# TensorE transposes instead of diagonal products: the B term of a selective scan on one core

## The chip, the cores and the metric

One Trainium2 chip; the program runs on one of its cores. The metric is the device time of one execution in microseconds, and the median of three runs is given. The core has five engines that run side by side, each through its own queue in order, and that wait for one another by semaphores: TensorE (PE, whose weight loads have a row of their own, PEld), VectorE (DVE), ScalarE (ACT), GpSimd (POOL) and SyncE (SP), which here only issues DMAs.

## The reference

The reference runs four layers over x of shape (4, 64, 64, 128), all in fp32. Layers 0, 1 and 3 are state-space blocks: a norm, a projection to 256 channels, a 3x3 depthwise convolution and SiLU, and then a selective scan in four directions (K = 4) over the 4096 positions of each image, with N = 16 states a channel. Layer 2 is a gated block without a scan. The scan is what matters here, cut to its core:

```python
def step(h, t):
    x_t, d_t, B_t, C_t = t
    h = jnp.exp(d_t[..., None] * A) * h + (d_t * x_t)[..., None] * B_t[:, :, None, :]
    return (h, jnp.einsum('bkdn,bkn->bkd', h, C_t))
```

So each state n needs, for every channel and position, a decay exp(delta*A), an input (delta*x)*B_n, a running recurrence along the positions, a product with C_n, and a sum over n.

## The kernel before, in words

The 4096 positions are cut into chunks of 512 (`CH`), channels lie on 128 partitions in two halves m. There are 12 turns (two pairs of images, three scan layers, one image a turn), each with 4 directions of 8 chunks: 384 chunks. A chunk has 8 periods: a period is one channel half and one group of four states (`place`, L879, picks both), so there are 3072 periods, and nearly all of the time is made of them.

In one period, states 0 and 1 of the group are side 0 and states 2 and 3 side 1. The recurrence is a VectorE scan (`scan`, L918), four a period, 512 positions each. The two sides get their input (delta*x)*B in two ways:

- Side 0 (`diagonals` L885, `pair_db` L895). delta*x stands transposed in SBUF (`duT`, positions on partitions). ScalarE builds diagonal matrices of B: ident times a column of B, 128x128, for each of four blocks of positions and each of two states, interleaved in one tile `diag`. TensorE multiplies `duT` by the diagonals: four products of 128x256 a period, into the PSUM tile `dbp` of two banks, in which the two states alternate element by element. The scans read it with a step of two.
- Side 1 (`lift` L915, L1048, L1049). ScalarE copies delta*x into a PSUM tile `dv` ("lifts" it). VectorE multiplies it by two rows of B, which a DMA has spread over all partitions (`bb`). The second product is written in place; the first goes into the other one of two `dv` tiles, and that one becomes the target of the next lift when its scan has read it.

Round this: ScalarE makes the decays (`decay` L903, two instructions a side) and saves the last column of a scan as the state for the next chunk (`save`). GpSimd multiplies the scans' results by C (`times_c` L934, 128x1024 each, twice a period, and in every second period adds the two sides). TensorE sums these over n into `yp` by products with ident (`add_up` L940). `leave` (L955) adds `yp` to the output when a half of a chunk is done.

The order on each queue is the order of the program text; nothing is moved by a scheduler. The loop over periods (from L985) sets it. In period i it issues the decay of side 0 of the next period (`then`), the save of the last one, the two scans of side 0, `times_c`, in even periods one `add_up`, `pair_db` of the next period, the decay of side 1 of the next period, the save, the two products at L1048 and L1049, the two scans of side 1, `times_c`, `lift` of the next period, half of a later group's diagonals, and two or three `add_up` of the period before. So TensorE's products for period i+1 are issued in the middle of period i, and the `add_up` calls of period i-1 near the end of period i. One more thing shapes this order: TensorE's `add_up` waits for GpSimd, which comes after VectorE.

Two other streams are woven in. `prologue` (L814) prepares the next chunk: loads, small products, delta, delta*x on GpSimd (L859), its transposes on TensorE (L865) and ScalarE's copies into `duT` (L867). It is cut by `yield` into ten steps, and `PIECES` says at which of the 16 half periods of a chunk the next step is issued. `other` feeds in the steps of the work between layers (norms, convolution, projections), spread by costs.

Of the kernel before, what the change touches and what calls it, by code (L numbers as in the profile page):

```python
# [13 lines left out]
F32 = mybir.dt.float32  # L14
AF = mybir.ActivationFunctionType
# [10 lines left out]
CH = 512  # L26
NCH = L // CH
RPC = CH // W
P = 128
WP = W + 2  # L30

CQ = 4
# [1 line left out]
PAIRED = (0, 2, 4, 6)  # L34


PIECES = (0, 3, 4, 6, 8, 9, 10, 11, 12, 13)


_VSS = [  # L40
# [58 lines left out]
def vss_stack_kernel(ctx: ExitStack, tc: tile.TileContext, x: bass.AP, weights, out: bass.AP, n_batch=B, layers=(0, 1, 2, 3)):  # L99
# [6 lines left out]
    nc = tc.nc  # L106
# [4 lines left out]
    ident = const.tile([P, P], F32, name="ident")  # L111
# [14 lines left out]
    for i in layers:  # L126
# [14 lines left out]
        t = const.tile([P, small_n + VSS_N - tail_at], F32, name=f"w{i}")  # L141
# [27 lines left out]
    def cols(c):  # L169
        return slice(c * CH, (c + 1) * CH)  # L170
# [596 lines left out]
    for turn, (e, i) in enumerate(turns):  # L767

        for nth, k in enumerate((1, 3, 0, 2) if turn else (0, 1, 3, 2)):
            for ci in range(NCH):  # L770
                s = SimpleNamespace(turn=turn, e=e, v=wt[i], layer=i, nth=nth, k=k, ci=ci)
                s.c = NCH - 1 - ci if k >= 2 else ci
                s.columns, s.back = k % 2 == 1, k >= 2
                s.end = 0 if s.back else CH - 1
                s.step = slice(None, None, -1 if s.back else 1)
                s.first, s.last = ci == 0, ci == NCH - 1
                s.flip = len(chunks) % 2
                s.diag, s.cb, s.bb, s.h, s.hc = {}, {}, {}, {}, {}
                chunks.append(s)
    per_turn = K * NCH  # L780

# [27 lines left out]
    def scans(pool, ring, deep, psum):  # L809
# [4 lines left out]
        def prologue(s):  # L814


            lane, v = lanes[s.e % 2], s.v
            s.xs = ring.tile([P, 2, CH], F32, tag="xs", name="xs")
            nc.sync.dma_start(out=s.xs, in_=(lane.x_col if s.columns else lane.x_row)[:, :, cols(s.c)])
            if s.first:  # L820
                s.dt = pool.tile([R, DI], F32, tag="dt", name="dt_w")
                nc.sync.dma_start(out=s.dt, in_=weights[s.layer][1][:, s.k * DI : (s.k + 1) * DI])


            s.xd_d = lane.xd[s.k % 2][s.c]
            s.xd = pool.tile([2 * NX, CH], F32, tag="xd", name="xd")
            if s.back:
                nc.sync.dma_start(out=s.xd[:NX], in_=s.xd_d[1])
            yield
            if s.back:  # L830
                yield
            else:
                ps = psum.tile([P, CH], F32, tag="misc", name="ps_x")
                for m in range(2):
                    nc.tensor.matmul(ps[: 2 * NX], v["xp"][:, s.k % 2, m, :], s.xs[:, m], start=(m == 0), stop=(m == 1))
                yield
                nc.scalar.copy(s.xd, ps[: 2 * NX])
            s.delta = pool.tile([P, 2, CH], F32, tag="delta", name="delta")
            halves = (s.flip, 1 - s.flip)
            for m in halves:  # L840
                ps = psum.tile([P, CH], F32, tag="misc", name="ps_dt")
                nc.tensor.matmul(ps, s.dt[:, m * P : (m + 1) * P], s.xd[:R], start=True, stop=True)  # L842
                yield
                func = AF.Identity if m == halves[0] else AF.Softplus
                nc.scalar.activation(s.delta[:, m], ps, func, bias=v["dtb"][:, s.k, m : m + 1])  # L845
            m = halves[0]
            nc.scalar.activation(s.delta[:, m], s.delta[:, m], AF.Softplus)  # L847
            nc.scalar.preload_act_table_set("natural_log_exp_and_others")
            ps = psum.tile([P, 4, NX], F32, tag="misc", name="ps_bt")
            for j in range(4):  # L850
                nc.tensor.transpose(ps[:, j, :], s.xd[:NX, j * P : (j + 1) * P], ident[:NX, :NX])
            yield
            if not s.back:
                nc.sync.dma_start(out=s.xd_d.rearrange("k r t -> (k r) t"), in_=s.xd)
            s.bt = pool.tile([P, 4, N], F32, tag="bt", name="bt")
            nc.scalar.copy(s.bt, ps[:, :, R : R + N])
            s.du = pool.tile([P, 2, CH], F32, tag="du", name="du")
            for m in halves:
                nc.gpsimd.tensor_mul(s.du[:, m], s.delta[:, m], s.xs[:, m])  # L859
                yield  # L860
            s.duT = pool.tile([P, 4, 2, P], F32, tag="duT", name="duT")
            for m in halves:
                ps = psum.tile([P, 4, P], F32, tag="misc", name="ps_duT")
                for j in range(4):
                    nc.tensor.transpose(ps[:, j, :], s.du[:, m, j * P : (j + 1) * P], ident)  # L865
                yield
                nc.scalar.copy(s.duT[:, :, m, :], ps)  # L867
            yield
# [10 lines left out]
        def place(s, i):  # L879


            q = i // 2
            return q, (i + q + s.flip) % 2

        def diagonals(s, q, half):  # L885

            if half == 0:
                s.diag[q] = pool.tile([P, 4, P, 2], F32, tag="diag", name="diag")
            for t in (2 * half, 2 * half + 1):
                for j in range(2):  # L890
                    nc.scalar.activation(  # L891
                        s.diag[q][:, t, :, j], ident, AF.Copy, scale=s.bt[:, t, CQ * q + j : CQ * q + j + 1]
                    )

        def pair_db(s, i):  # L895
            q, m = place(s, i)
            s.db = psum.tile([P, CH, 2], F32, tag="dbp", name="dbp")
            for t in range(4):
                nc.tensor.matmul(  # L899
                    s.db[:, t * P : (t + 1) * P, :], s.duT[:, t, m, :], s.diag[q][:, t], start=True, stop=True  # L900
                )

        def decay(s, i, side):  # L903
            q, m = place(s, i)
# [8 lines left out]
        dv = [psum.tile([P, CH], F32, name=f"dv{j}") for j in range(2)]  # L913

        def lift(s, i):  # L915
            nc.scalar.copy(dv[i % 2], s.du[:, place(s, i)[1]])  # L916

        def scan(s, i, side, j, da, db):  # L918
            q, m = place(s, i)
            if j == 0:  # L920
                s.h[i, side] = deep.tile([P, 2, CH], F32, tag="h", name="h")
            n = CQ * q + 2 * side + j
            init = 0.0 if s.first else s.state[:, m, n : n + 1]
            nc.vector.tensor_tensor_scan(  # L924
                s.h[i, side][:, j, s.step], da[:, j, s.step], db[:, s.step], init, ALU.mult, ALU.add
            )
# [13 lines left out]
        def add_up(s, i, *calls):  # L940


            q, m = place(s, i)
            start, end = (0, 7) if m == s.flip else (1, 6)
            for call in calls:
                opens = i == start and call == (2 if i in PAIRED else 0)
                if opens:
                    setattr(s, f"yp{m}", psum.tile([P, CH], F32, tag=f"yp{m}", name="yp"))
                side, j = divmod(call, 2)
                closes = i == end and call == 3  # L950
                nc.tensor.matmul(getattr(s, f"yp{m}"), ident, s.hc[i, side][:, j], start=opens, stop=closes)  # L951
                if closes:
                    full.append((s, m))
# [15 lines left out]
        for step in sum([combine(0, psums)] + opening[:4], []):  # L969
            step()  # L970
        s = chunks[0]
        pro = prologue(s)
        for _ in pro:
            pass
        for q, half in ((0, 0), (0, 1), (1, 0)):
            diagonals(s, q, half)
        spread(s, 0, 0)
        spread(s, 0, 1)
        pair_db(s, 0)
# [1 line left out]
        da = [decay(s, 0, side) for side in range(2)]  # L981
# [3 lines left out]
        for at, (s, i) in enumerate(periods):  # L985
            then = periods[at + 1] if at + 1 < len(periods) else None
            if i == 0:
                nxt = chunks[at // 8 + 1] if at // 8 + 1 < len(chunks) else None
# [14 lines left out]
            def piece(number):  # L1003

                if nxt and number in PIECES:
                    next(pro)
# [21 lines left out]
                save(*before, 1)  # L1028
            if spreads:
                spread(*spreads, 0)  # L1030
            scan(s, i, 0, 0, da[0], s.db[:, :, 0])
            other(0)
            scan(s, i, 0, 1, da[0], s.db[:, :, 1])
            times_c(s, i, 0)

            if before and i % 2 == 0:
# [10 lines left out]
            du, db = dv[i % 2], dv[1 - i % 2]  # L1047
# [3 lines left out]
            other(2)  # L1051
            scan(s, i, 1, 1, da[1], du)
            times_c(s, i, 1)
            if then:
                lift(*then)

            q, half = (i + 2 + i % 2) // 2, 1 - i % 2
            if q < 4:
                diagonals(s, q, half)
            elif nxt:  # L1060
                diagonals(nxt, q - 4, half)
            if i < 2 and full:
                leave(*full.pop(0))
            if before:
                add_up(*before, *((2, 3) if i % 2 else (1, 2, 3)))
            piece(2 * i + 1)
            other(3)
            da = da_next
# [103 lines left out]
```

## Time and profile before

| what | value |
|---|---|
| time, median of three runs | 22066.67 us (22064.29 to 22081.29) |
| span of the profiled execution | 22070.4 us |
| mean granted TensorE clock in it | 0.963 |
| PE / DVE / ACT / POOL busy | 89% / 88% / 84% / 87% |
| periods; mean length of one | 3072; 22070.4 / 3072 = 7.18 us |

The page gives no other time for the profiled execution than its span, which lies within the three runs; span and time are taken as one here. Busy time is the share of the span in which an engine's instructions are running. A group's row gives an instruction by its line and engine, what it writes and reads, its count, the busy time and the mean duration of one, and after the bar how long the engine stood idle before it and what ended that. A product of fp32 operands stands in the trace as two rows with two weight loads, a transpose as one, so the four products of a period at L899 are eight rows.

### The profile page before, as it was taken

How to read it: one execution, taken by the hardware profiler on the slowest of the kernel's cores; microseconds unless marked ns; L12 is line 12 of the kernel's file. 1: busy time of each engine (PE TensorE's matmuls, PEld its weight loads, DVE VectorE, ACT ScalarE, POOL GpSimd, SP SyncE). 2: the span in 40 equal slices, each digit the busy share in tenths (PEclk: the TensorE clock that was granted, in tenths of full speed). 3: DMA queues.
4: the chain of work that ended last, by engine and by line, in shares of the span. 5: the costliest groups of instructions: out<-in, count | busy, mean ns of one | idle time of the engine just before them, and what ended most of it. 6: DMA issues, size and time to landing. Idle time of an engine off the chain costs nothing. (4 is left out here: it accounts for less than half of the span.)

```text
span 22070.4 us, 216982 instructions
## 1 busy us (share of the span) xinstructions
PE 19694.9 (89%) x58234; PEld 10511.8 (48%) x58234; DVE 19479.8 (88%) x20186; ACT 18587.9 (84%) x40022; POOL 19266.5 (87%) x8862
## 2 busy tenths in 40 slices
PE   7898998898889889889989988989988988898897
PEld 3444444444444444444444444444444444444443
DVE  5999999999888888899889899989988888889996
ACT  6888888888888888888888888888888888888887
POOL 5999899899888888888889888988988888889996
PEclk9999999999999999999999999999999999999999
DMA  4444444444335434434534544444443453354342
GB/s 109 147 149 146 135 144 149 136 139 151 130 131 139 142 128 140 146 133 145 144 138 144 145 141 140 141 147 134 142 149 127 137 143 137 131 140 145 140 144 101
DMA packets 2437559, 3060.10 MB, mean 139 GB/s; under 512 B 1753840, under 2 KB 1790064, under 8 KB 2238192
## 3 DMA queue, kind: packets, MB, share of 16 engines
q1 hardware_dynamic: 2436336, 3046.22, 44.4%
q8 instruction: 472, 7.73, 0.1%
q14 instruction: 751, 6.15, 0.1%
HBM read 2784.41 MB, written 261.49 MB: 138 GB/s over the span
## 5 line engine op out<-in xcount | busy, mean ns | idle before, releaser
L936 POOL TENSOR_TENSOR hc<-h,cb 128x1024 f32<-128x1024 f32 x6144 | 14399.4, 2363 | 2276.5 <-DVE h L924 1113.1
L951 PE MATMUL yp<-hc,ident 128*128 128x512 f32 x18432 | 9062.1, 618 | 688.3 <-POOL hc L938 546.8
L908 ACT ACTIVATE da<-delta,w 128x512 f32<-128x512 f32 x12288 | 8148.0, 713 | 543.5 <-DVE h L924 530.5
L924 DVE TENSOR_TENSOR_SCAN h<-da,state,dbp 128x512 f32<-128x512 f32 x5376 | 6573.3, 1262 | 818.9 <-PE dbp L899 576.0
L899 PE MATMUL dbp<-diag,duT 128*128 128x256 f32 x24576 | 6012.6, 388 | 652.4 <-DVE h L924 560.1
L924 DVE TENSOR_TENSOR_SCAN h<-da,state,dv 128x512 f32<-128x512 f32 x5376 | 6589.4, 1264 | 0.0
L899 PEld LDWEIGHTS dbp<-diag,duT 128*128 128x128 f32 x24576 | 4675.2, 193 | 2921.3 <-issue 1673.1
L951 PEld LDWEIGHTS yp<-hc,ident 128*128 128x128 f32 x18432 | 3483.6, 196 | 4999.1 <-issue 3656.8
L891 ACT ACTIVATE diag<-ident,bt 128x128 f32<-128x128 f32 x12288 | 3952.1, 402 | 0.0
L938 POOL TENSOR_TENSOR hc<-hc 128x1024 f32<-128x1024 f32 x1536 | 3624.1, 2359 | 120.4
L1048 DVE TENSOR_TENSOR dv<-dv,bb 128x512 f32<-128x512 f32 x3072 | 2088.3, 680 | 945.9 <-ACT dv L916 730.3
L916 ACT COPY dv<-du 128x512 f32<-128x512 f32 x3072 | 1799.1, 586 | 984.6 <-DVE h L924 977.1
L1049 DVE TENSOR_TENSOR dv<-dv,bb 128x512 f32<-128x512 f32 x3072 | 2118.4, 690 | 0.0
L444 PE MATMUL gap<-halo,cw 128*128 128x512 f32 x3456 | 1750.8, 604 | 5.9 <-DVE cen L281 2.2
L924 DVE TENSOR_TENSOR_SCAN h<-da,dbp 128x512 f32<-128x512 f32 x768 | 891.1, 1202 | 250.7 <-PE dbp L899 166.9
L859 POOL TENSOR_TENSOR du<-delta,xs 128x512 f32<-128x512 f32 x768 | 979.9, 1276 | 31.8 <-ACT delta L847 31.8
L842 PE MATMUL ps_dt<-xd,dt_w 8*128 8x512 f32 x1536 | 881.2, 654 | 130.2 <-ACT delta L845 78.2
L932 ACT COPY state<-h 128x2 f32<-128x2 f32 x5376 | 964.3, 179 | 0.0
L444 PEld LDWEIGHTS gap<-halo,cw 128*128 128x128 f32 x3456 | 628.1, 191 | 654.8 <-issue 617.8
L924 DVE TENSOR_TENSOR_SCAN h<-da,dv 128x512 f32<-128x512 f32 x768 | 893.8, 1204 | 0.0
L845 ACT ACTIVATE delta<-ps_dt,w 128x512 f32<-128x512 f32 x768 | 524.9, 683 | 103.0 <-PE ps_dt L842 98.2
L865 PEld LDWEIGHTS ps_duT<-ident,du 128*128 128x128 f32 x3072 | 383.7, 142 | 321.9 <-issue 255.8
(122 smaller groups left out, 11686.6 us busy)
## 6 DMA issues: line engine op xcount, KB each, us to landing
cb<-xd_d SPq DMA_DIRECT2D x1536, 1024.0 KB
bb<-xd_d SPq DMA_DIRECT2D x1536, 512.0 KB
xs<-x_row_d SPq DMA_DIRECT2D x192, 512.0 KB
xs<-x_col_d SPq DMA_DIRECT2D x192, 512.0 KB
x_col_d<-down SPq DMA_DIRECT2D x192, 256.0 KB
x_row_d<-wide SPq DMA_DIRECT2D x96, 512.0 KB
y_d<-y_sb SPq DMA_DIRECT2D x96, 512.0 KB
y<-y_d SPq DMA_DIRECT2D x96, 512.0 KB
```

What stands on the lines that cost most here:

```text
L444: nc.tensor.matmul(z.ps, z.cw[:, m, t, :], z.halo[c][:, dy : dy + RPC, dx : dx + W], start=(t == 0), stop=(t == 8),)
L859: nc.gpsimd.tensor_mul(s.du[:, m], s.delta[:, m], s.xs[:, m])
L891: nc.scalar.activation(s.diag[q][:, t, :, j], ident, AF.Copy, scale=s.bt[:, t, CQ * q + j : CQ * q + j + 1])
L899: nc.tensor.matmul(s.db[:, t * P : (t + 1) * P, :], s.duT[:, t, m, :], s.diag[q][:, t], start=True, stop=True)
L908: nc.scalar.activation(da[:, j], s.delta[:, m], AF.Exp, scale=s.v["a"][:, s.k, m, n : n + 1])
L916: nc.scalar.copy(dv[i % 2], s.du[:, place(s, i)[1]])
L924: nc.vector.tensor_tensor_scan(s.h[i, side][:, j, s.step], da[:, j, s.step], db[:, s.step], init, ALU.mult, ALU.add)
L936: nc.gpsimd.tensor_mul(hc, s.h[i, side], s.cb[i // 2][:, 2 * side : 2 * side + 2, :])
L938: nc.gpsimd.tensor_add(hc, hc, s.hc[i, 0])
L951: nc.tensor.matmul(getattr(s, f"yp{m}"), ident, s.hc[i, side][:, j], start=opens, stop=closes)
L1048: nc.vector.tensor_mul(db, du, s.bb[i // 2][:, 0])
L1049: nc.vector.tensor_mul(du, du, s.bb[i // 2][:, 1])
```

## The change

On side 0, the diagonals go. `diagonals` becomes `scaled`: for each state, ScalarE multiplies the transposed delta*x itself by the column of B, both channel halves in one instruction of 128x256, four instructions a state. `pair_db` then has TensorE transpose the scaled tile back, four transposes of 128x128 a state, each state into a PSUM tile of its own, one bank each (`db0`, `db1`), and the scans read them without a step.

On side 1, `lift` is no longer ScalarE's copy but four TensorE transposes of the unscaled `duT` into the same `dv` tile. It is issued after the `add_up` calls of the period before, no longer straight after the last scan.

The scaled tiles of the next chunk need `duT`, which the diagonals did not, so `PIECES` moves the prologue's steps earlier: the last is issued in the middle of period 5 instead of at the end of period 6. `du` has one buffer instead of two, `dub` has three where `diag` had two.

```diff
-PIECES = (0, 3, 4, 6, 8, 9, 10, 11, 12, 13)
+PIECES = (0, 2, 3, 4, 5, 6, 7, 8, 9, 10)
...
-            s.du = pool.tile([P, 2, CH], F32, tag="du", name="du")
+            s.du = pool.tile([P, 2, CH], F32, tag="du", name="du", bufs=1)
...
-        def diagonals(s, q, half):
-            if half == 0:
-                s.diag[q] = pool.tile([P, 4, P, 2], F32, tag="diag", name="diag")
-            for t in (2 * half, 2 * half + 1):
-                for j in range(2):
-                    nc.scalar.activation(
-                        s.diag[q][:, t, :, j], ident, AF.Copy, scale=s.bt[:, t, CQ * q + j : CQ * q + j + 1]
-                    )
+        def scaled(s, q, j):
+            duB = s.dub[q, j] = pool.tile([P, 4, 2, P], F32, tag="dub", name="dub", bufs=3)
+            for t in range(4):
+                nc.scalar.activation(
+                    duB[:, t], s.duT[:, t], AF.Copy, scale=s.bt[:, t, CQ * q + j : CQ * q + j + 1]
+                )
 
         def pair_db(s, i):
             q, m = place(s, i)
-            s.db = psum.tile([P, CH, 2], F32, tag="dbp", name="dbp")
-            for t in range(4):
-                nc.tensor.matmul(
-                    s.db[:, t * P : (t + 1) * P, :], s.duT[:, t, m, :], s.diag[q][:, t], start=True, stop=True
-                )
+            for j in range(2):
+                s.db[j] = psum.tile([P, CH], F32, tag=f"db{j}", name="db")
+                for t in range(4):
+                    nc.tensor.transpose(s.db[j][:, t * P : (t + 1) * P], s.dub[q, j][:, t, m, :], ident)
...
         def lift(s, i):
-            nc.scalar.copy(dv[i % 2], s.du[:, place(s, i)[1]])
+            m = place(s, i)[1]
+            for t in range(4):
+                nc.tensor.transpose(dv[i % 2][:, t * P : (t + 1) * P], s.duT[:, t, m, :], ident)
...
-            scan(s, i, 0, 0, da[0], s.db[:, :, 0])
+            scan(s, i, 0, 0, da[0], s.db[0])
             other(0)
-            scan(s, i, 0, 1, da[0], s.db[:, :, 1])
+            scan(s, i, 0, 1, da[0], s.db[1])
...
             times_c(s, i, 1)
-            if then:
-                lift(*then)
 
             q, half = (i + 2 + i % 2) // 2, 1 - i % 2
             if q < 4:
-                diagonals(s, q, half)
+                scaled(s, q, half)
             elif nxt:
-                diagonals(nxt, q - 4, half)
+                scaled(nxt, q - 4, half)
             if i < 2 and full:
                 leave(*full.pop(0))
             if before:
                 add_up(*before, *((2, 3) if i % 2 else (1, 2, 3)))
+            if then:
+                lift(*then)
```

More of the change, by code (lines that the diff above doesn't have):

```diff
@@ L777, in vss_stack_kernel @@
                 s.flip = len(chunks) % 2
-                s.diag, s.cb, s.bb, s.h, s.hc = {}, {}, {}, {}, {}
+                s.dub, s.db, s.cb, s.bb, s.h, s.hc = {}, {}, {}, {}, {}, {}
                 chunks.append(s)
@@ L1053, in scans @@
             times_c(s, i, 1)
-            if then:
-                lift(*then)
             q, half = (i + 2 + i % 2) // 2, 1 - i % 2
             if q < 4:
-                diagonals(s, q, half)
+                scaled(s, q, half)
             elif nxt:
-                diagonals(nxt, q - 4, half)
+                scaled(nxt, q - 4, half)
             if i < 2 and full:
```

## The prediction

> **What bounds the kernel now.** I read the busy shares first, then the groups of instructions with their idle time, then VectorE's own waits, then single stretches of the timeline. The groups:
>
> ```profile
> span 22070.4 us, 216982 instructions
> ...
> PE 19694.9 (89%) x58234; PEld 10511.8 (48%) x58234; DVE 19479.8 (88%) x20186; ACT 18587.9 (84%) x40022; POOL 19266.5 (87%) x8862
> ...
> L951 PE MATMUL yp<-hc,ident 128*128 128x512 f32 x18432 | 9062.1, 618 | 688.3 <-POOL hc L938 546.8
> L908 ACT ACTIVATE da<-delta,w 128x512 f32<-128x512 f32 x12288 | 8148.0, 713 | 543.5 <-DVE h L924 530.5
> L924 DVE TENSOR_TENSOR_SCAN h<-da,state,dbp 128x512 f32<-128x512 f32 x5376 | 6573.3, 1262 | 818.9 <-PE dbp L899 576.0
> L899 PE MATMUL dbp<-diag,duT 128*128 128x256 f32 x24576 | 6012.6, 388 | 652.4 <-DVE h L924 560.1
> L924 DVE TENSOR_TENSOR_SCAN h<-da,state,dv 128x512 f32<-128x512 f32 x5376 | 6589.4, 1264 | 0.0
> ...
> L891 ACT ACTIVATE diag<-ident,bt 128x128 f32<-128x128 f32 x12288 | 3952.1, 402 | 0.0
> ...
> L916 ACT COPY dv<-du 128x512 f32<-128x512 f32 x3072 | 1799.1, 586 | 984.6 <-DVE h L924 977.1
> ```
>
> No engine is the bound alone: four stand at 84 to 89% and wait for one another. VectorE and GpSimd do no less work after the change, so the span cannot fall under about 19480 us, and what can be won lies in VectorE's 22070.4 - 19479.8 = 2590.6 us of idle time. Its waits:
>
> ```profile
> DVE h L924 <- PE dbp L899: 742.8, 557, 8.6
> DVE dv L1048 <- ACT dv L916: 730.3, 328, 7.5
> DVE dv L1048 <- DMA bb<-xd_d: 196.1, 64, 6.3
> ```
>
> The change touches the makers of the first two: 1473 us. TensorE's 89% flatters it (ends are modelled and overlap). Prices come from the spacing inside runs of one kind:
>
> ```profile
> 157.25 1.09 PE L865 MATMUL ps_duT<-ident,du 128*128 128x128 f32 x4 [1.49 <-ACT bt L856]
> ...
> 10043.91 0.60 PE L865 MATMUL ps_duT<-ident,du 128*128 128x128 f32 x4
> ...
> 10045.03 1.34 ACT L908 ACTIVATE da<-delta,w 128x512 f32<-128x512 f32 x2
> ...
> 10045.20 1.89 PE L899 MATMUL dbp<-diag,duT 128*128 128x256 f32 x8
> ...
> 10048.04 1.28 ACT L891 ACTIVATE diag<-ident,bt 128x128 f32<-128x128 f32 x4
> ```
>
> **The change, part by part.**
>
> *VectorE.* The scan that reads `dbp` with a step of two takes 1262 ns, the one that reads `dv` without a step 1264. Dropping the step is worth 0.
>
> *TensorE's work.* Four transposes take 0.60 us with 0.273 us for a single one (its row's median), so each further one costs (0.60 - 0.273)/3 = 0.109 us. A period's `pair_db` takes 1.89 us in eight rows; eight transposes take 0.273 + 7 x 0.109 = 1.04. The lift adds 4 x 0.109 = 0.44. Net 0.41 us a period less, some 1260 us of TensorE time in 3072 periods, mostly off the path.
>
> *ScalarE's work.* Diagonals cost 1.28/4 = 0.32 us each at 128 elements, decays 1.34/2 = 0.67 at 512, so 256 elements lie between; by the line 0.32 + 0.35 x 128/384 = 0.44. Four a period: +0.46 us. The lift's 0.59 goes. Net -0.13 us a period, some -400 us, off the path. More important, ScalarE no longer stands at the lift waiting for a scan (977.1 us). What is late there next is the decay, which waits for a scan as well (530.5 us now).
>
> *(a) The scan's wait for TensorE, 742.8 us.* The first scan needs four transposes in `db0`, ready 0.60 us after they begin, where it needed 1.89: 1.29 us sooner. `db0` is also free for its writer one scan (1.2 us) earlier. Going through the trace's 3072 first scans, the idle times before them, each cut by 1.29 us, would leave 36%. So 64% goes: -480 us. Ends: all of it (-743), and half (-370) if the saving is the 0.85 us of the shorter run alone.
>
> *(b) VectorE's wait for ScalarE's lift, 730.3 us,* goes: -730. ScalarE's lateness then acts through the scaled tiles; see (d).
>
> *(c) The new wait: VectorE at L1048 for TensorE's lift.* It stands in TensorE's queue behind the last `add_up` calls, which wait for GpSimd (546.8 us of TensorE's idle time ends there), and behind woven-in products. Behind the lift stand the next `add_up` and `pair_db`. For each period I read from the trace when the last `add_up` ended and when VectorE was ready for L1048. With 0.60 us for the lift added, it would have been late in 2001 of 3071 periods, by 3190 us in all. So everything hangs on how much earlier TensorE gets there. Moved x us earlier, but never before GpSimd's result allows, the sum is 1855 us for x = 0.85, 1439 for 1.25, 1112 for 1.7, 939 for 2.07; GpSimd alone leaves 389. For x I take 0.85 (shorter products) + 1.2 (earlier start) - 0.44 (the lift before it in the queue) = 1.6 to 1.7, so 1112. The sum counts each period for itself, yet a late lift also holds VectorE back and makes the next less late; I take 0.72 of it, a choice: +800 us. Ends 389 and 1855.
>
> *(d) Smaller things.* The ten prologue steps move up to four half periods. On GpSimd's queue `du` (1276 ns, twice a chunk) passes three products with C, on SP's queue the store of `xd` passes spreads of B and C; the counts stay, and each consumer is still two half periods behind its producer. The cover is that distance: if it is gone, waits like those now seen (104.9 us for ScalarE's copy of `duT` behind L865, 248.3 for its copy of `ps_x`) could double: 0 to +250. `du` with one buffer is rewritten a chunk after its last reader: 0. With three `dub` buffers, ScalarE's writing waits for this period's `pair_db`, usually over: 0 to +100. Against that, ScalarE's idle at the lift is free for late decays, worth up to the 104.7 us that VectorE waits for them. Together 0, ends -100 and +350.
>
> *(e) The clock.* The rows at 157 and 10043 us are the same four transposes at half and at full granted clock. In the clock's record half clock holds for 1650 us of the span, in steps of 3.41 us. A full-clock step with less than 1.0 us of streaming on TensorE is always followed by half clock; between 1.0 and 1.4 us it is in 67% of 103 steps without transposes and in none of 14 with 0.3 us or more of them. So here transposes count as work. Shrinking the products by 0.62 lifts the steps below 1.3 us from 6% to 8% of 6441: 130 more, at most 1.3 us of lost TensorE time each, 170 us, mostly hidden: taken as 0 within (d)'s ends.
>
> A rule of the Trainium skill speaks against this change: "TensorE: Matmul & The Clock Gate", Part 4, says that transpose mode does not count as TensorE being busy, so full clock does not engage. By it the sum would be that of the clock rival below; by the 14 steps it would not.
>
> **Sum.** 22070 - 480 - 730 + 800 = 21660 us. The profiled span, 22070.4, is 4 us from the median of the runs, so nothing is added.
>
> **Rivals.**
>
> *More is won* (20990 to 21300). TensorE runs ahead so far that only GpSimd's 389 us remain and all of (a) goes: 22070 - 743 - 730 + 389 = 20986. For it: 0.41 us less TensorE work in every period, which adds up through a backlog. Against: GpSimd would then be busy 19266/20986 = 92%.
>
> *The lift is the new bound, slower.* One mechanism: TensorE in order, `lift` behind `add_up`. If TensorE is usually behind (only 904 of 3072 `pair_db` now start within 0.35 us of their scan), the earlier start is worth nothing and x is 0.85: 0.72 x 1855 = 1340, with (a) -370: 22070 - 370 - 730 + 1340 = 22310; unscaled 22820. It decides from a new wait above 1210 us.
>
> *The clock falls, slower.* If transposes do not count as work, the steps with under 1.3 us rise from 6% to 24%: some 1160 more, about 0.8 us lost in each, 930 us of TensorE time. Half to all of it on the path: 22130 to 22590. The 14 steps speak against it.
>
> *Nothing is left*, within 0.2%: the new wait happens to equal what goes, 1210 us.
>
> **How the numbers follow.** The three runs differ by 17 us; about 0.2%, 44 us, is what a measurement can tell from no change. Chances: the forecast 0.43 (its own range 21350 to 21950), more won 0.19, nothing left 0.07, the lift as bound 0.22, the clock 0.09. So faster 0.62, same 0.07, slower 0.31. The range 21000 to 22450 leaves out the far ends of three cases, about 0.2.
>
> **What would show it.** L1048's wait changes its releaser from ScalarE to TensorE and is near 800 us: under 500 the first rival holds, over 1210 the second. The first scan's wait for `db` is under 270 us. Transposes at 273 ns, scaled tiles near 510 ns mean duration (402 and 713 are their neighbours) and spaced 0.44 us. TensorE's granted clock at 0.95 to 0.96; under 0.90 the clock rival holds. VectorE's and GpSimd's busy times unchanged within 1%. The forecast is wrong first if x is: that is the least certain number here.

## The result

The changed kernel takes 22218.22 us (median of 4 runs, 22205.21 to 22236.35) against 22065.48 for the kernel before: a ratio of 1.0069, interval 1.0055 to 1.0083. It is slower by 153 us where 406 us less was forecast. The sign was wrong; the time lies in the range, near the rival in which the lift is the new bound. The profiled execution has a span of 22234.6 us.

The page of the changed kernel, its busy shares and the groups that answer to those shown before:

```profile
span 22234.6 us, 240297 instructions
...
PE 19006.2 (85%) x70522; PEld 10073.3 (45%) x70522; DVE 19464.5 (88%) x20186; ACT 18368.0 (83%) x36950; POOL 19271.7 (87%) x8862
...
L950 PE MATMUL yp<-hc,ident 128*128 128x512 f32 x18432 | 9350.3, 632 | 1131.9 <-POOL hc L937 1125.0
L905 ACT ACTIVATE da<-delta,w 128x512 f32<-128x512 f32 x12288 | 8167.8, 714 | 1331.2 <-DVE h L923 1309.0
L923 DVE TENSOR_TENSOR_SCAN h<-da,state,db 128x512 f32<-128x512 f32 x5376 | 6558.7, 1258 | 282.7 <-PE db L898 170.4
L923 DVE TENSOR_TENSOR_SCAN h<-da,state,dv 128x512 f32<-128x512 f32 x5376 | 6586.8, 1263 | 10.4 <-ACT da L905 10.0
...
L889 ACT ACTIVATE dub<-duT,bt 128x256 f32<-128x256 f32 x12288 | 5227.8, 497 | 464.7 <-PE db L898 461.4
L898 PE MATMUL db<-ident,dub 128*128 128x128 f32 x24576 | 3506.2, 281 | 656.1 <-DVE h L923 556.8
...
L1047 DVE TENSOR_TENSOR dv<-dv,bb 128x512 f32<-128x512 f32 x3072 | 2099.4, 683 | 1839.9 <-PE dv L915 1642.3
```

TensorE and ScalarE have less to do (689 and 220 us less busy), VectorE and GpSimd the same, and still the span grows. VectorE's idle time is 22234.6 - 19464.5 = 2770 us, against 2591. Its waits in the changed kernel:

```profile
DVE dv L1047 <- PE dv L915: 1642.3, 832, 11.0
DVE h L923 <- PE db L898: 186.3, 92, 7.8
DVE dv L1047 <- DMA bb<-xd_d: 183.4, 45, 8.9
```

The balance: the scan's wait for TensorE falls by 557 us, the wait for ScalarE's copy by 730, all other waits together by 176; the new wait for TensorE's lift brings 1642. That makes +179 us of idle time; 15 us less busy time leaves the 164 us between the two spans.

The new wait is not spread evenly. Added up from the trace by the place of a period in its chunk (a period is counted from its first scan; mean us in a period; "first scan" is the idle time before it, "L1048" that before the first product with `bb`, L1047 in the changed kernel):

| period | length, before | first scan | L1048 | length, after | first scan | L1047 |
|---|---|---|---|---|---|---|
| 0 | 7.57 | 0.16 | 0.37 | 7.45 | 0.05 | 0.47 |
| 1 | 7.31 | 0.23 | 0.17 | 7.19 | 0.03 | 0.14 |
| 2 | 7.20 | 0.10 | 0.36 | 7.20 | 0.00 | 0.67 |
| 3 | 7.21 | 0.66 | 0.09 | 8.64 | 0.30 | 1.77 |
| 4 | 7.41 | 0.56 | 0.46 | 6.83 | 0.18 | 0.44 |
| 5 | 7.29 | 0.60 | 0.68 | 6.76 | 0.14 | 0.34 |
| 6 | 6.38 | 0.35 | 0.16 | 6.92 | 0.12 | 0.80 |
| 7 | 6.67 | 0.13 | 0.18 | 6.49 | 0.02 | 0.17 |

Five of the eight periods are shorter now and one as long. Period 6 is 0.54 us longer, and period 3 alone 1.43 us, 549 us in 384 chunks. One such period 3, from the timeline of the changed kernel (start, duration, engine):

```profile
10625.71 1.04 PE L898 MATMUL db<-ident,dub 128*128 128x128 f32 x8
...
10626.67 1.12 PE L842 MATMUL ps_dt<-xd,dt_w 8*128 8x512 f32 x2
10626.71 2.43 DVE L923 TENSOR_TENSOR_SCAN h<-da,state,db 128x512 f32<-128x512 f32 x2
...
10627.73 1.13 PE L444 MATMUL gap<-halo,cw 128*128 128x512 f32 x2
...
10628.69 2.74 PE L950 MATMUL yp<-hc,ident 128*128 128x512 f32 x6
...
10631.26 0.60 PE L915 MATMUL dv<-ident,duT 128*128 128x128 f32 x4
...
10631.90 0.70 DVE L1047 TENSOR_TENSOR dv<-dv,bb 128x512 f32<-128x512 f32 x1 [2.76 <-PE dv L915]
```

TensorE works without a pause from 10625.71 on: the transposes that this period's first two scans read, a prologue product, a convolution tap, three sums for `yp`, and only then the lift for which VectorE has been waiting since its second scan ended at 10629.14. In the order of the program these instructions, the lift too, belong to period 2, an even one: they are issued one period ahead of the scans that read them. In this stretch no engine waits for the sums, 2.74 us.

### The profile page after: what moved, and what is told of

The parts are those of the page before. It is cut to its first block, busy times and chain, and to the rows that moved or that the text cites. A ratio compares the mean times of both kernels' runs of the same rounds, so it can differ in the third digit from the quotient of the medians.

```text
span 22234.6 us, 240297 instructions
## 1 busy us (share of the span) xinstructions
PE 19006.2 (85%) x70522; PEld 10073.3 (45%) x70522; DVE 19464.5 (88%) x20186; ACT 18368.0 (83%) x36950; POOL 19271.7 (87%) x8862
## 5 line engine op out<-in xcount | busy, mean ns | idle before, releaser
L950 PE MATMUL yp<-hc,ident 128*128 128x512 f32 x18432 | 9350.3, 632 | 1131.9 <-POOL hc L937 1125.0
L923 DVE TENSOR_TENSOR_SCAN h<-da,state,db 128x512 f32<-128x512 f32 x5376 | 6558.7, 1258 | 282.7 <-PE db L898 170.4
L889 ACT ACTIVATE dub<-duT,bt 128x256 f32<-128x256 f32 x12288 | 5227.8, 497 | 464.7 <-PE db L898 461.4
L898 PE MATMUL db<-ident,dub 128*128 128x128 f32 x24576 | 3506.2, 281 | 656.1 <-DVE h L923 556.8
L898 PEld LDWEIGHTS db<-ident,dub 128*128 128x128 f32 x24576 | 2894.5, 144 | 2289.0 <-issue 1190.0
L1047 DVE TENSOR_TENSOR dv<-dv,bb 128x512 f32<-128x512 f32 x3072 | 2099.4, 683 | 1839.9 <-PE dv L915 1642.3
L915 PEld LDWEIGHTS dv<-ident,duT 128*128 128x128 f32 x12288 | 1612.9, 147 | 1819.3 <-issue 1540.0
L1048 DVE TENSOR_TENSOR dv<-dv,bb 128x512 f32<-128x512 f32 x3072 | 2115.8, 689 | 0.0
L915 PE MATMUL dv<-ident,duT 128*128 128x128 f32 x12288 | 1929.1, 281 | 36.0 <-DVE h L923 35.7
L923 DVE TENSOR_TENSOR_SCAN h<-da,db 128x512 f32<-128x512 f32 x768 | 887.6, 1197 | 39.1 <-ACT da L905 18.7
L444 PEld LDWEIGHTS gap<-halo,cw 128*128 128x128 f32 x3456 | 559.5, 193 | 357.6 <-issue 335.6
```

Source lines behind the costliest of these rows:

```text
L444: nc.tensor.matmul(z.ps, z.cw[:, m, t, :], z.halo[c][:, dy : dy + RPC, dx : dx + W], start=(t == 0), stop=(t == 8),)
L889: nc.scalar.activation(duB[:, t], s.duT[:, t], AF.Copy, scale=s.bt[:, t, CQ * q + j : CQ * q + j + 1])
L898: nc.tensor.transpose(s.db[j][:, t * P : (t + 1) * P], s.dub[q, j][:, t, m, :], ident)
L915: nc.tensor.transpose(dv[i % 2][:, t * P : (t + 1) * P], s.duT[:, t, m, :], ident)
L923: nc.vector.tensor_tensor_scan(s.h[i, side][:, j, s.step], da[:, j, s.step], db[:, s.step], init, ALU.mult, ALU.add)
L1047: nc.vector.tensor_mul(db, du, s.bb[i // 2][:, 0])
```

## The experiments

The theories. A: the lift is late because of its place behind `add_up` in TensorE's queue. B: TensorE as a whole is short of time, since its clock is at half for 2583 us of the span (1650 before). C: the earlier prologue steps crowd periods 2 and 3. All times below are medians; "against before" is the difference to the kernel before, measured beside it on the same chip, and the ratio to it stands with its interval.

| kernel | B term | lift | prologue | median us | against before | ratio (interval) |
|---|---|---|---|---|---|---|
| after | scaled | TensorE, behind sums | early | 22218 | +153 | 1.0069 (1.0055 to 1.0083) |
| lift_first | scaled | TensorE, ahead of sums | early | 21789 | -265 | 0.988 (0.9863 to 0.9896) |
| scaled_copy_lift | scaled | ScalarE's copy | early | 22116 | +51 | 1.0023 (1.0013 to 1.0032) |
| early_prologue | diagonals | ScalarE's copy | early | 22271 | +217 | 1.0097 (1.0082 to 1.0112) |
| diag_lift_first | diagonals | TensorE, ahead | old | 22236 | +182 | 1.0082 (1.0067 to 1.0097) |
| diag_lift_last | diagonals | TensorE, behind | old | 22631 | +576 | 1.026 (1.0245 to 1.0276) |
| odd_first | scaled | ahead in odd periods | early | 22093 | +38 | 1.0018 (1.0008 to 1.0027) |
| even_first | scaled | ahead in even periods | early | 22005 | -50 | 0.9977 (0.9967 to 0.9987) |

### The lift's place: lift_first

```diff
             times_c(s, i, 1)
+            if then:
+                lift(*then)
...
             if before:
                 add_up(*before, *((2, 3) if i % 2 else (1, 2, 3)))
-            if then:
-                lift(*then)
```

> The changed kernel with one thing moved: the lift's four transposes are issued straight after the last products with C, ahead of the add_up calls, where the copy stood before. Theory A (the lift's place behind add_up in TensorE's in-order queue is the cause): VectorE's wait for the lift falls from 1642 us to under 500 and the time to about 21300 us (21000 to 21700). Theory B (TensorE as a whole is short of time, by its half clock): the wait stays above 1200 us and the time between 22050 and 22250. Theory C (the prologue's earlier steps crowd periods 2 and 3): as B, with the waits still gathered in period 3.

Measured 21789 us, 429 us under the changed kernel and 1.2% under the kernel before. VectorE's waits in lift_first:

```profile
DVE h L923 <- PE db L898: 528.9, 350, 8.6
DVE dv L1047 <- PE dv L915: 353.2, 200, 7.7
DVE dv L1047 <- DMA bb<-xd_d: 278.1, 78, 8.6
```

The wait for the lift falls from 1642 us to 353, as theory A says. Of these 1289 us, 343 come back as a wait for the next period's transposes, which TensorE reaches later, and some 490 as smaller waits: for the decays (75 to 207 us), for the rows of B (183 to 278), for GpSimd (17 to 99) and others. That is why the time did not fall to 21300. B falls as the main cause: TensorE has the same work, and only its order changed. Half clock still holds for 2064 us of this span; that is 519 us less than in the changed kernel, so a part of the gain may be the clock's. The next pair of runs shows the same price of the place at an equal clock.

### The lift alone, with diagonals: diag_lift_last and diag_lift_first

```diff
         def lift(s, i):
-            nc.scalar.copy(dv[i % 2], s.du[:, place(s, i)[1]])
+            m = place(s, i)[1]
+            for t in range(4):
+                nc.tensor.transpose(dv[i % 2][:, t * P : (t + 1) * P], s.duT[:, t, m, :], ident)
```

This is the kernel before with TensorE's lift, in diag_lift_last moved behind the `add_up` calls, in diag_lift_first left in the copy's place.

> The kernel before (diagonals, old PIECES) with the lift alone changed: four transposes of duT on TensorE behind the add_up calls. Theory A: TensorE is busier here than in the changed kernel, so the wait for the lift is at least the 1642 us seen there, against 730 for the copy; time 22800 to 23500 us. Theory C: without the moved prologue the late place costs little; 21950 to 22250 us. Theory B: four more transposes a period (0.44 us) on a TensorE at nearly full clock: 22200 to 22600 us.

> The kernel before with the lift on TensorE, straight after the last products with C, ahead of add_up. Theory A: the wait for the lift falls under 500 us, part comes back as a later pair_db (742.8 us grows to about 1000); time 21750 to 22000 us. Theory B: TensorE carries 0.44 us more in every period and everything on it is later; 22200 to 22600 us. Theory C says nothing here beyond B.

Measured 22631 and 22236 us. The late place costs 395 us here, close to the 429 with the scaled tiles. The mean granted clock is 0.974 in the one and 0.976 in the other, and the prologue is the old one, so the late place needs neither half clock nor crowding to hurt. VectorE's longest waits in diag_lift_last and in diag_lift_first:

```profile
DVE dv L1050 <- PE dv L918: 2141.2, 1363, 11.2
DVE h L926 <- PE dbp L899: 198.9, 150, 17.0
```

```profile
DVE h L926 <- PE dbp L899: 1114.2, 825, 17.2
DVE dv L1050 <- PE dv L918: 315.9, 163, 8.3
```

The wait moves between two consumers of the same TensorE queue. Theory A had the first too high (22800 to 23500) and the second too low (21750 to 22000). The first lies between B's range and A's; for the second B's range is the one that holds. With the longer diagonal products, 0.44 us more on TensorE in every period does cost, 182 us.

### The prologue: early_prologue, late_prologue, first_and_late, room_moved and the moved step

Early_prologue is the kernel before with the changed `PIECES` alone:

```diff
-PIECES = (0, 3, 4, 6, 8, 9, 10, 11, 12, 13)
+PIECES = (0, 2, 3, 4, 5, 6, 7, 8, 9, 10)
```

> The kernel before with the changed kernel's PIECES alone. Theory A and B: the time stays within 60 us of 22066. Theory C: VectorE's waits grow in periods 2 and 3 and the time rises by 150 to 700 us.

Measured 22271 us, +217: the earlier steps have a price, and the prediction had taken 0. The period means show where: period 3 grows from 7.21 to 8.53 us and period 2 from 7.20 to 7.83, while 4 and 5 shrink to 6.90 and 6.71. VectorE's wait for `dbp` rises from 743 to 978 us. ScalarE's wait at `delta` for TensorE's `ps_dt`, one step before, rises from 98 to 425 us.

Late_prologue spreads the steps in the changed kernel again, by making the next chunk's first scaled tile a period later; first_and_late does the same in lift_first:

```diff
-PIECES = (0, 2, 3, 4, 5, 6, 7, 8, 9, 10)
+PIECES = (0, 2, 3, 5, 7, 8, 9, 10, 11, 12)
...
-            elif nxt:
+            elif nxt and i > 5:
+                if i == 6:
+                    scaled(nxt, 0, 0)
                 scaled(nxt, q - 4, half)
```

> The changed kernel with the prologue's steps spread again: the next chunk's first scaled tile is made in period 6 with the second one, no longer in period 5, so PIECES can be (0, 2, 3, 5, 7, 8, 9, 10, 11, 12). Lift still behind add_up. Early_prologue put the price of the crowded steps at 217 us on the kernel before. Theory A+C (place and crowding add up): the wait for the lift falls from 1642 us to about 1350, mostly in period 3, and the time from 22218 to about 22030 us (21950 to 22130). Theory A alone (the late lift hides the crowding): 22170 to 22250 us.

> Lift ahead of add_up and the prologue spread again, both in the changed kernel. If the two causes add up: 21789 - 190, about 21600 us (21530 to 21680). If the crowding is repaired by the early lift already: 21740 to 21820 us.

Both expectations fell: 22292 us (1.0106, interval 1.009 to 1.0123) and 21910 us (0.9933, 0.9918 to 0.9948), 74 and 121 us slower than without the edit. In late_prologue the wait for the lift does fall, from 1642 to 1456 us, but the one for `db` rises from 186 to 487. In first_and_late period 3 shrinks to 7.08 us as hoped (8.00 in lift_first), but period 4 grows from 6.84 to 7.91, and TensorE now stands 506 us at the transposes of B for ScalarE's softplus. The jam moved with the step; the eight scalings in one period are a second change in this edit, so it does not price the spreading alone.

Room_moved leaves the prologue and moves other woven-in work out of periods 2 and 3 of lift_first:

```diff
-ROOM = (2.8, 1.5, 1.5, 1.5, 1.0, 1.0, 1.5, 1.8)
+ROOM = (2.8, 1.5, 1.0, 1.0, 1.5, 1.5, 1.5, 1.8)
```

> Lift_first with the woven-in work moved from periods 2 and 3 to 4 and 5 (the shares of a chunk's work between layers, 1.5, 1.5, 1.0, 1.0 become 1.0, 1.0, 1.5, 1.5), steps of the prologue unmoved. If it is the sum of work in periods 2 and 3 that crowds: 21600 to 21700 us against 21789. If it is the half-period distance between dependent prologue steps: within 60 us of 21789.

21807 us (0.9886, 0.9871 to 0.9901), no different from lift_first: taking a third of the other work out of these periods wins nothing. First_pieces_moved (on lift_first) and copy_pieces_moved (on scaled_copy_lift, below) put the one free half period elsewhere:

```diff
-PIECES = (0, 2, 3, 4, 5, 6, 7, 8, 9, 10)
+PIECES = (0, 1, 2, 4, 5, 6, 7, 8, 9, 10)
```

> Lift_first with the one free half period of the prologue between its third and fourth step instead of its first and second: PIECES (0, 1, 2, 4, 5, 6, 7, 8, 9, 10). If ScalarE standing at delta for TensorE's ps_dt (486 us in lift_first, 98 in the kernel before) is what the crowded prologue costs: that wait falls under 200 us and the time to 21620 to 21730. If the price lies elsewhere (softplus and its two table loads one period earlier): 21740 to 21850. If xs has not landed yet: above 21850, with TensorE waiting at ps_x.

> Scaled_copy_lift with the same moved step. As above, measured from scaled_copy_lift: 60 to 170 us less if the wait at delta is the price, within 60 us if not.

21774 us (0.9868, 0.9853 to 0.9882) and 22099 us (1.0013, 1.0003 to 1.0023): 16 and 17 us less, inside the noise of the first and at its edge for the second. In the first, ScalarE's 486 us at `delta` fall to 4, but its wait at `xd`, one step earlier, rises from 85 to 375 us. So removing the wait at `delta` by itself wins nothing; it moved. A reading that fits, and that no run shows, is that the group of softplus, two table loads (1.28 us each in the timeline) and the products before and after them jams a period wherever it lies, and that the old order had it spread better. Which part of it costs the 217 us stays open.

### The products alone: scaled_copy_lift

```diff
         def lift(s, i):
-            m = place(s, i)[1]
-            for t in range(4):
-                nc.tensor.transpose(dv[i % 2][:, t * P : (t + 1) * P], s.duT[:, t, m, :], ident)
+            nc.scalar.copy(dv[i % 2], s.du[:, place(s, i)[1]])
```

The lift stands in its old place, `du` has two buffers and `duT` one.

> The changed kernel with the lift given back to ScalarE, as the copy of du in its old place (du gets two buffers again, duT one). Only the products with B and the prologue are then changed. If the parts add up as in the kernels with diagonals, where the lift on TensorE cost 182 us ahead of add_up against the copy: 21789 - 182, about 21610 us (21500 to 21720), with VectorE's wait for the copy near 500 us. If with shorter products TensorE has room for an early lift and ScalarE, with its longer scaling, is late with the copy: 21789 to 22000 us.

22116 us: the second of the two expectations was nearer, and the measurement lies above even that. Its busy shares:

```profile
PE 18046.5 (82%) x58234; PEld 8835.4 (40%) x58234; DVE 19454.4 (88%) x20186; ACT 19852.7 (90%) x40022; POOL 19272.0 (87%) x8862
```

ScalarE is the busiest engine now, and stands only 144 us at the decays for a scan (1309 in the changed kernel): it has little slack left, and VectorE waits 678 us for its copy and 655 for `db`. Against early_prologue the new products win 0.0097 - 0.0023 of the time, some 165 us; the lift on TensorE, ahead of the sums, wins another 316 (+51 to -265). So both halves of the change pay, and the parts do not add up as in the kernels with diagonals: there the same lift cost 182 us. The likely reason is that ScalarE had room there and TensorE had not, but no run tests it alone, and the clock is a rival: half clock holds for 3501 us of the span of scaled_copy_lift (granted clock 0.921), for 1729 in early_prologue (0.961) and for 2064 in lift_first (0.953). With the lift's transposes TensorE has more to do and yet spends less time at half clock.

### GpSimd or the plain length of the queue: one_sum_first, odd_first, even_first

In the changed kernel the lift stands in odd periods behind two sums that wait for GpSimd's added sides, in even ones behind three sums. One_sum_first is first_and_late with the one sum whose input is a period old put ahead of the lift, in even periods:

```diff
+            if before and i % 2 == 0:
+                add_up(*before, 1)
             if then:
                 lift(*then)
...
-                add_up(*before, *((2, 3) if i % 2 else (1, 2, 3)))
+                add_up(*before, 2, 3)
```

> As first_and_late, and in even periods the first of the three late add_up calls, whose input is a period old, is issued before the lift, so that TensorE has 0.86 us of work while the lift waits for the scan (832 us of such waits in lift_first). Theory A in the form 'only what waits for GpSimd must stand behind the lift': 50 to 150 us below first_and_late. Theory 'TensorE's time before the lift is what counts': the same or up to 150 us above it.

21924 us (0.9938, 0.9924 to 0.9953) against 21910: one sum ahead of the lift gains nothing, although its input is ready. VectorE's wait for the lift rises from 242 to 367 us. Odd_first and even_first move the lift of the changed kernel ahead of the sums in one kind of period each (`if then and i % 2 == 1` and `== 0` at the early place, the rest at the late one):

> The changed kernel with the lift ahead of add_up in odd periods alone, where it otherwise stands behind the two sums that wait for GpSimd's added sides; in even periods it stays behind three sums. In the changed kernel's trace 723 us of VectorE's wait belong to these lifts (382 of them), 399 us of it with TensorE idle for GpSimd. Theory A1 (waiting for GpSimd is the cause): most of the 430 us that the early place is worth is won here, 21780 to 21920 us. Theory A2 (the queue's plain length, three sums of 0.86 us and the crowded prologue, is the cause): about 100 to 200 us are won, 22020 to 22120.

> The mirror: the lift ahead of add_up in even periods alone, where three sums stand before it and none of VectorE's 926 us of wait (520 lifts) has TensorE idle for GpSimd. Theory A1: little is won, 22120 to 22230 us. Theory A2: most of the 430 us, 21790 to 21950.

22093 and 22005 us: 115 us won against the changed kernel in odd periods, 203 in even ones, 418 with both (each taken against the kernel before that was measured beside it). Odd_first lies in A2's range; even_first, at 22005, lies between the two ranges. About half is won in the even periods, where no wait has TensorE idle for GpSimd: that half is A2's, the plain length of the queue. In the odd ones 399 of the 723 us of wait have TensorE idle for GpSimd, and how much of the 115 us is GpSimd's is not parted; 100 us come only with both. The period means agree: the lift that period 3 reads is issued in period 2, an even one, and in odd_first period 3 still has 1.93 us of wait at L1047, in even_first 0.47.

## Why the prediction was wrong

- **(a) The scan's wait for TensorE:** the number came near, 743 us became 186 (480 were to go and 557 went), but not by the mechanism alone that was given for it. Diag_lift_last, with the old products, has 199 us too, and lift_first, with the new ones, 529: while VectorE stands at a late lift, TensorE's products for the next scan get done. The shorter products alone took 323 us off this wait (978 in early_prologue, 655 in scaled_copy_lift). So the near hit is partly luck.
- **(b) The wait for ScalarE's copy:** right, all 730 us went. ScalarE stood longer elsewhere, at the decays (530 to 1309 us), as foretold.
- **(c) The new wait for the lift:** this term failed. 800 us were put in, 1642 came, in 832 periods. The mechanism was named, and so was the price from which it decides: above 1210 us the second rival holds. That a late lift belongs to its place is shown by lift_first (353 us of wait, -429 us of time) and by the pair with diagonals (395 us).

  The step that failed is x, how much earlier TensorE gets to the lift. It was taken as 1.6 to 1.7 us (the terms give 1.61; 1112 us belongs to 1.7). In the traces, the last `add_up` of a period ends on average 7.16 us after the second scan of side 0 of that period before the change, and 6.28 us after it in the changed kernel: by this measure x was 0.88.

  The 1.2 us of earlier start could not be added in full to the 0.85 of shorter products. `db0` is free one scan earlier, but the four transposes into `db1` still wait for the second scan, and all of TensorE's queue waits with them: in the changed kernel's trace TensorE stands idle at that point 489 times, 293 us. So `pair_db` ends on average 2.42 us after the second scan where it ended 3.48 us after it, 1.06 us sooner. The same diff also puts work in TensorE's way, the earlier products of the prologue and 932 us more of half clock; what these took from x no run shows.

  The factor of 0.72, a choice, failed as well. At x = 0.88 the prediction's own unscaled sums, 1855 us at 0.85 and 1439 at 1.25, give an estimate of some 1820 us, and 1642 is 0.9 of it.
- **(d) The prologue:** the prologue's part was taken as 0, with all of (d) between -100 and +350; on the kernel before it measures +217. "Each consumer is still two half periods behind its producer" holds for `du` and its transposes. It does not hold for the steps before: `delta` follows its product by one half period where it followed by two.
- **(e) The clock:** the reading was right, the amount too small. Half clock rose from 7.5% to 11.6% of the span, not by two points. Transposes do count as work, as the trace before had hinted with 14 steps. Take streaming as the time of TensorE's rows by their spacing at full clock (0.43 us for 512 columns, 0.11 for a transpose). In the changed kernel, of the full-clock steps of 3.41 us with 0.8 to 1.0 us of streaming by products, all 16 with hardly any transposes (under 0.05 us) are followed by half clock, and none of the 173 with 0.85 us or more of them.
- **The Trainium skill:** "TensorE: Matmul & The Clock Gate", Part 4, says that full clock does not engage for transpose mode. Here the measurement decides against it, for fp32 transposes of 128x128.
- **Prices:** VectorE's step of two is worth nothing (1258 ns without it, 1262 with it). Eight transposes take 1.04 us, as worked out; a scaled tile's instruction has a mean of 497 ns (510 foretold), and four of them take 1.70 us (1.76). From the changed kernel's timeline:

```profile
10504.90 1.04 PE L898 MATMUL db<-ident,dub 128*128 128x128 f32 x8
...
10506.19 1.70 ACT L889 ACTIVATE dub<-duT,bt 128x256 f32<-128x256 f32 x4
```

- **The rivals:** the lift as bound is what happened, at 22234 us in the profiled execution and not 22310: 302 us more of the new wait, 187 more won from (a), 176 less of other waits and 15 of busy time. That the sum came so near is luck, since its misses cancel. The clock did not decide: the mean granted clock is 0.942, where its rival was to show under 0.90.

## What to carry to other kernels

When an operation moves to another engine, look at what stands before it in that engine's queue at the moment its consumer wants it, and put it ahead of work that nobody waits for yet: here the whole change was worth +153 us or -265 us by the place of the same four transposes alone. Cost what the diff moves on the same queue (here a prologue) with the same care as what it adds. When an earlier start is counted as slack, ask which instruction of the group is the last to be free: here the first tile could start a scan earlier, the second could not, and what is issued behind both gained little. A factor that shrinks such a sum needs a row to support it.

## What the runs showed that was not expected

- The parts of this change do not add: the lift on TensorE, ahead of the sums, costs 182 us beside diagonals and wins 316 beside scaled tiles. ScalarE is 84% busy with its copy in the one and 90% in the other; that its load decides is likely, not shown, and half clock differs too.
- The place of the lift sets another wait as well: with the lift late, the scan's wait for its input is 199 us beside diagonals and 186 beside scaled tiles; with the lift early, 1114 and 529.
- A ScalarE instruction of 128x256 that multiplies by a column costs 0.425 us in a row of four (1.70 us), where one of 128x128 costs 0.32.
- The best versions run, lift_first and first_pieces_moved (0.988 and 0.9868), beat both kernels. Both keep the whole change and place the lift ahead of the sums; the second also moves one step of the prologue, and the two are not clearly apart.
